# A decoder layer: the order of TensorE's transposes among the projections beside them

## The chip, the cores and the metric

The kernel runs on one core of a Trainium2 chip. The metric is the device time in microseconds, the median of three runs. A core has engines that work side by side, each through its own instructions in order: TensorE (PE, matmuls and transposes, results in PSUM), VectorE (DVE), ScalarE (ACT), GpSimd (POOL) and SyncE (SP, which issues DMAs). Semaphores make one wait for another.

## What is computed

A decoder layer on x of shape 4 x 512 x 512 with a context of the same shape, fp32. LN is a layer normalization over the last axis; there are 16 heads of 32.

```python
x = x + attn(LN(x))                 # causal self-attention, 16 heads
x = x + cross(LN(x), ctx, ctx)      # causal, no projections: keys and values are ctx
y = LN(x)
top2 = top_k(y @ W_gate.T, 2)
x = x + relu(y @ W_up.T) @ W_down.T + sum(softmax(top2)) * (y @ W_expert)

# attn: q, k, v = y @ w.T + b;  softmax(mask(q k.T / sqrt(32))) v;  then @ o_w.T + o_b
# cross: a masked score is -10000, not -inf; the rest as in attn, without weights
```

## The kernel before, in words

**Rounds.** The loop over b runs through the four batches; below, a round is one b. A round does self-attention, the output projection with the norms of the cross query, cross-attention, and the feed-forward. Activations that are contracted next must lie with the feature on the partitions, so normalized rows (tiles `made[0..3]`, 128 rows each) are turned by TensorE: `columns` (L243) issues four 128x128 transposes for each of two tiles into one pair of PSUM banks, and one ScalarE copy takes them to SBUF (`cqT`, the cross query, L257 with a scale; `fT`, the feed-forward input, L255).

**PSUM.** All PSUM tiles come from one pool of four buffers of two banks (`pair`, L65). A new tile takes a buffer that is free in the order of the program, and its first writer waits until the engine that read the old contents is done.

**The order of the work is written by hand** for TensorE, VectorE, ScalarE and GpSimd (L836): each runs what the program issues for it, in that order. SyncE's DMAs are issued by the same steps.

**Two passes of an attention.** `with_maxima` (L781) makes the first: for each of 4 groups of 4 heads, and in it for each of three units of query blocks, (0,1), (2) and (3), `Attention.maxima` (L267) computes scores (sm), ScalarE copies them (L292), GpSimd masks the diagonal (L298), and VectorE finds each row's largest value (`largest`, L310). `split` (L323) cuts the maxima of a group into bf16 parts, `rows` (L334) turns them: four transposes on TensorE (mt, L338) and a VectorE copy into `mrow` (L344). `attend` (L811) makes the second pass: scores again (sc, L370), minus the maxima by a matmul with `mrow` (L381), exponentials on ScalarE (L402), and the products with the values (pv, L429). It begins with units (0), (1), (2,3) of group 0. The last group's `rows` are called inside it.

**Filling.** Between the units of the first pass TensorE does other projections' matmuls: `steps`, through the generator `matmuls` (L775), which yields behind each matmul. How many come into a unit follows from the due time in L797: the total shared out by the units' costs and rounded. VectorE's work on a unit's scores (`jobs`) is issued one job behind each of the next unit's fill matmuls, and what is left behind the last. At a unit with block 3, from the second group on, `rows` of the group before is issued first, ahead of the fill, and its copy heads the jobs:

```python
            if i[-1] == NT - 1 and g > 0:
                jobs = a.rows(g - 1) + jobs
            due += total * cost[n] / sum(cost)
```

With the numbers of steps here, a unit with block 3 that calls `rows` gets 2 fill matmuls in the cross-attention of rounds 0 and 2 and in the self-attention of round 3, 2, 3 and 2 in the cross-attention of round 3, and 3 or 4 elsewhere. In the trace each fp32 matmul of the code is two instructions.

**What fills what.** In rounds 0 to 2 the query, key and value projections of the next batch (`query_key`, `value`) stand in the cross part, in round 3 the feed-forward of round 2: `gates` (share, which writes the logits' PSUM tile lg, L708, and gate), `ups`, `downs`; `experts` stand where they are put by L875 to L885. Round 3's self-attention is filled by one batch's experts alone.

**Around the change.** Behind the output projection come three steps, then all 16 transposes of the cross query, then the first pass:

```python
            run(steps[:3])
            norm_cross(e, made)
```

Behind the cross-attention, `filler` is value of the next batch (rounds 0 to 2) or experts (round 3): its first step, then `add_cross` (transposes tp_x, adding, norms), its other three steps, and `norm_ffn` (L681) with 16 transposes. The feed-forward's input tile in round 2 takes the buffer of `xnT`, which value reads.

Of the kernel before, what the change touches and what calls it, by code (L numbers as in the profile page):

```python
# [9 lines left out]
F32 = mybir.dt.float32  # L10
# [8 lines left out]
P = 128  # L19
# [7 lines left out]
def decoder_layer(  # L27
# [22 lines left out]
    B, S, D = x.shape  # L50
    NH = 16
    HD = D // NH
    NT = S // P
    NC = D // P
    HG = P // HD
    NE = wgate.shape[-1]
    SCALE = 1.0 / math.sqrt(HD)

    const = ctx.enter_context(tc.tile_pool(name="const", bufs=1))
    act = ctx.enter_context(tc.tile_pool(name="act", bufs=1))  # L60
# [4 lines left out]
    def pair(name):  # L65

        return ps.tile([P, 2, S], F32, tag="ps", name=name)


    def load_x(b):  # L70
        xb = act.tile([P, NT, D], F32, tag="x", name=f"x_{b}", bufs=2)
        src = x[b].rearrange("(t p) d -> p t d", p=P)
        for t in range(NT):
            queue = nc.scalar if b == 0 and t % 2 else nc.sync
            queue.dma_start(out=xb[:, t, :], in_=src[:, t, :])
        return xb
# [62 lines left out]
    for r in range(HG):  # L139
# [26 lines left out]
        fill=BIG,  # L166
# [6 lines left out]
    for n in range(2):  # L173
        t = const.tile([P, NT, P], BF16, name=f"parts{n}")
# [3 lines left out]
    def keep_warm(name, count):  # L178

        out = pair(name)  # L180
        for n in range(count):
            nc.tensor.matmul(
                out[:, 0, :P], lhsT=ident, rhs=ident, start=True, stop=True
            )
# [58 lines left out]
    def columns(srcs, dst, t, tp, scale=None, warm=0):  # L243

        for n, src in enumerate(srcs):
            if warm:
                keep_warm(f"warm_{t}_{n}", warm)
            for c in range(NC):
                nc.tensor.transpose(
                    tp[:, n, c * P : (c + 1) * P], src[:, c * P : (c + 1) * P], ident  # L250
                )
        to = dst[:, :, t * P : (t + 2) * P].rearrange("p c (n q) -> p c n q", q=P)
        come = tp.rearrange("p n (c q) -> p c n q", q=P)
        if scale is None:
            nc.scalar.copy(to, come)  # L255
        else:
            nc.scalar.mul(to, come, scale)  # L257
# [251 lines left out]
    def norm_in(b, given=None):  # L509

        e = Entry()
        e.b, e.x, e.xn_t = b, given, None
        src = x[b].rearrange("(t p) d -> p t d", p=P)

        def source(t):
            if given is not None:
                return given[:, t, :]
            xi = work.tile([P, D], F32, tag="xin", name=f"xin_{b}_{t}")
            nc.sync.dma_start(out=xi, in_=src[:, t, :])
            return xi  # L520

        made, norms = layernorms(source, f"a{b}")

        def turn(t):
            if e.xn_t is None:
                e.xn_t = act.tile([P, NC, S], F32, tag="xn_t", name=f"xnT_{b}")
            columns(
                [made[t], made[t + 1]],
                e.xn_t,
                t,  # L530
                pair(f"tp_a{b}_{t}"),
                warm=0 if b else 2,
            )

        return e, norms, [(lambda t=t: turn(t)) for t in (0, 2)]

    def add_bias(e):
        for t in range(NT):
            nc.gpsimd.tensor_tensor(e.x[:, t, :], e.x[:, t, :], bo_sb, ALU.add)
# [49 lines left out]
    def value(e):  # L589
        b, made = e.b, {}  # L590
        e.v = act.tile([P, NT, D], F32, tag="v", name=f"v_{b}")

        def one(t):
            if t % 2 == 0:
                made[0] = pair(f"pm_v{b}_{t}")
            yield from project(made[0][:, t % 2, :], e.xn_t, wv_sb, t)
            if t % 2 == 1:
                nc.vector.tensor_tensor(
                    e.v[:, t - 1 : t + 1, :],
                    made[0],  # L600
                    bv_sb.unsqueeze(1).to_broadcast([P, 2, D]),
                    ALU.add,
                )

        return [(lambda t=t: one(t)) for t in range(NT)]
# [47 lines left out]
        run(norms)  # L653
        return made

    def norm_cross(e, made):
        b = e.b
        e.cq_t = act.tile([P, NC, S], F32, tag="o_t", name=f"cqT_{b}")
        for t in (0, 2):
            columns(made[t : t + 2], e.cq_t, t, pair(f"tp_q{b}_{t}"), SCALE)  # L660

    def add_cross(e, a):
        b = e.b
# [14 lines left out]
        run(norms)  # L678
        return made

    def norm_ffn(e, made):  # L681
        b = e.b
        e.f_t = act.tile(
            [P, NC, S], F32, tag="f_t" if b != B - 2 else "xn_t", name=f"fT_{b}"
        )
        for t in (0, 2):
            columns(made[t : t + 2], e.f_t, t, pair(f"tp_f{b}_{t}"))

    def ffn(e):
        b, f_t, made = e.b, e.f_t, {}  # L690
# [79 lines left out]
    def run(steps):  # L770
        for step in steps:
            for _ in step() or ():
                pass

    def matmuls(steps):  # L775

        for step in steps:
            yield from step() or ()
            yield

    def with_maxima(steps, a, first=0, norms=()):  # L781


        norms = list(norms)
        run(steps[:first])
        fill = matmuls(steps[first:])
        total = sum(1 if step.__name__ in ("share", "gate") else NC for step in steps[first:])
        units = [(g, i) for g in range(NC) for i in ((0, 1), (2,), (3,))]
        cost = [sum(k + 1.5 for k in i) for _, i in units]
        done, due, jobs = 0, 0.0, []  # L790
        for n, (g, i) in enumerate(units):
            new = a.maxima(g, i)
            if norms and n % 2 == 0:
                new.append(norms.pop(0))
            if i[-1] == NT - 1 and g > 0:
                jobs = a.rows(g - 1) + jobs
            due += total * cost[n] / sum(cost)  # L797

            while done < round(due):
                next(fill, None)  # L800
                done += 1
                run(jobs[:1])
                jobs = jobs[1:]
            run(jobs)
            jobs = new
        for _ in fill:
            pass
        run(jobs)
        return NC - 1
# [26 lines left out]
    with tc.manual_schedule(engines=BY_HAND):  # L836
        e, norms, turns = norm_in(0, x0)
        keep_warm("warm", 12)
        run(norms)
        run(turns)  # L840
        nc.gpsimd.tensor_scalar(bqs_sb, bq_sb, SCALE, None, ALU.mult)
        add_bias(e)
        between_self = query_key(e) + value(e)
        skip, between_cross, ahead = 3, [], []
        for b in range(B):
            more = b + 1 < B
            sa = Attention(e.q_t, e.k_t, e.v, False, f"s{b}")
            norms, turns = [], []
            if more:
                after, norms, turns = norm_in(b + 1)  # L850
            late = with_maxima(between_self, sa, skip, norms)
            if b == B - 1:
                e.x = load_x(b)
            attend(sa, late)
            if b > 0:
                add_bias(e)
            made = out_projection(e, sa, context(e) + turns)
            steps = (query_key(after) if more else []) + between_cross
            run(steps[:3])
            norm_cross(e, made)  # L860
            ca = Attention(e.cq_t, e.ck_t, e.cv, True, f"c{b}")
            ca.e = e
            late = with_maxima(steps[3:], ca)
            if b + 2 < B:
                after.x = load_x(b + 1)
            attend(ca, late)
            if more:
                cvs[b + 1] = load_cv(b + 1)
            filler = value(after) if more else ahead
            run(filler[:1])  # L870
            made = add_cross(e, ca)
            run(filler[1:])
            norm_ffn(e, made)
            gates, ups, downs, experts = ffn(e)
            if b + 3 < B:  # L875
                between_self, between_cross = gates[:1] + ups + gates[1:] + downs, experts
            elif b + 2 < B:
                between_self, between_cross = gates[:1] + ups + gates[1:] + downs, []
                ahead = experts
            elif more:  # L880
                between_self, ahead = ahead, experts
                between_cross = gates[:1] + ups + gates[1:] + downs
            else:
                run(gates[:1] + ups + gates[1:])
                run(downs[:2] + experts[:2] + downs[2:] + experts[2:])  # L885
            skip = 0
            if more:
                e = after
# [48 lines left out]
```

## Time and profile before

| what | value |
|---|---|
| median of 3 runs | 830.17 us (830.14 to 830.2) |
| the profiled execution | 829.93 us |
| its span, first to last instruction | 828.2 us |
| TensorE busy | 813.8 us, 98% |
| VectorE busy | 547.0 us, 66% |
| ScalarE busy | 397.9 us, 48% |
| GpSimd busy | 297.8 us, 36% |
| granted TensorE clock | 0.999 |

How to read it: the page names engines PE, DVE, ACT and POOL. A row of a timeline is: start in us, length in us, engine, line, operation, output<-inputs, shape, number of instructions, and in brackets idle time of the engine ahead of it with what ended it. A row of waits is: total us, times, longest. Matmuls overlap, and a row's length reaches to the modelled end of its last one, so starts are the surer measure. L310 is line 310 of the kernel before.

### The profile page before, as it was taken

The page shows a single profiled execution, that of the slowest core. Times are in us where ns is not written, and L with a number is a line of the kernel's source. Part 1 is how long each engine was busy: PE and PEld are TensorE (multiplying, and loading weights), DVE is VectorE, ACT ScalarE, POOL GpSimd, SP SyncE. Part 2 cuts the span into 40 slices and gives each one's busy share as a digit, 9 for nine tenths or more (in the row PEclk, how much of TensorE's full clock was granted, in tenths as well). Part 3 has the DMA queues.
Part 4 walks back from the last instruction along what each step waited for, and adds up shares of the span by engine and source line. Part 5 has one row for each costly group of instructions (what it writes and reads, how often), then busy time and mean ns, then how long its engine had stood idle before and what let it go on. Part 6 is the DMA issues. An engine that isn't in the chain of part 4 may idle for free.

```text
span 828.2 us, 14453 instructions
## 1 busy us (share of the span) xinstructions
PE 813.8 (98%) x5800; PEld 369.4 (45%) x5800; DVE 547.0 (66%) x937; ACT 397.9 (48%) x502; POOL 297.8 (36%) x549
## 2 busy tenths in 40 slices
PE   9999999999999999999999999999998999999998
PEld 7344444345444454334534444434543444444443
DVE  2578736877678834687858863687779835887511
ACT  2456526761546515556054651676166714574110
POOL 4434512442334732234233471244233643333100
PEclk9999999999999999999999999999999999999999
DMA  9600000001010000030100000000102000000101
GB/s 340 232 27 15 1 1 1 2 2 51 5 35 13 2 1 1 0 103 2 51 14 13 2 2 0 1 2 2 53 16 72 18 1 0 1 2 2 51 0 51
DMA packets 13539, 24.54 MB, mean 30 GB/s; under 512 B 1952, under 2 KB 1952, under 8 KB 13472
## 3 DMA queue, kind: packets, MB, share of 16 engines
q1 hardware_dynamic: 13184, 23.09, 8.2%
q8 instruction: 45, 0.74, 0.4%
q10 hardware_dynamic: 288, 0.52, 0.2%
q14 instruction: 22, 0.18, 0.1%
HBM read 19.42 MB, written 4.19 MB: 29 GB/s over the span
## 4 chain that ended last, share of the span: by engine, by line
PE 92%; ACT 3%; DVE 3%; issue 2%; DMA 0%; POOL 0%; ACTq 0%
PE pm_qk L233 12%; PE pv_c L429 9%; PE pm_u L233 7%; PE pm_d L221 7%; PE pm_v L221 7%; PE pm_o L638 7%; PE pm_e L221 6%; PE pv_s L429 6%; PE sm_c L280 6%; PE sc_s L370 5%; PE sc_c L370 5%; PE sm_s L280 5%; PE sc_s L381 1%; DVE nm_s L310 1%; PE sc_c L381 1%
## 5 line engine op out<-in xcount | busy, mean ns | idle before, releaser
L310 DVE TENSOR_REDUCE nm_c<-s_c 128x2 f32<-128x256 f32 (+3 forms) x128 | 96.3, 810 | 36.6 <-POOL s_c L298 36.6
L310 DVE TENSOR_REDUCE nm_s<-s_s 128x2 f32<-128x256 f32 (+3 forms) x128 | 96.6, 810 | 28.1 <-POOL s_s L298 28.1
L292 ACT COPY s_s<-sm_s 128x768 f32<-128x768 f32 (+1 forms) x96 | 78.9, 874 | 67.2 <-PE sm_s L280 50.9
L292 ACT COPY s_c<-sm_c 128x768 f32<-128x768 f32 (+1 forms) x96 | 78.9, 875 | 48.8 <-PE sm_c L280 34.5
L402 ACT ACTIVATE pt_c<-sc_c 128x768 f32<-128x768 f32 (+1 forms) x96 | 78.6, 883 | 28.7 <-PE sc_c L381 24.8
L298 POOL TENSOR_SCALAR_AFFINE_SELECT s_c<-s_c 128x256 f32<-128x256 f32 (+1 forms) x96 | 46.7, 487 | 119.1 <-ACT s_c L292 118.1
L404 POOL TENSOR_SCALAR_AFFINE_SELECT pt_c<-pt_c 128x256 f32<-128x256 f32 (+1 forms) x96 | 56.7, 598 | 71.0 <-ACT pt_c L402 70.1
L298 POOL TENSOR_SCALAR_AFFINE_SELECT s_s<-s_s 128x256 f32<-128x256 f32 (+1 forms) x96 | 46.9, 491 | 96.7 <-ACT s_s L292 95.7
L458 DVE TENSOR_TENSOR sum_s<-sum_s,pt_s 128x512 f32<-128x512 f32 (+1 forms) x72 | 63.2, 915 | 7.4 <-PE pv_s L429 6.4
L221 PE MATMUL pm_d<-wdown_sb,hT 128*128 128x512 f32 x128 | 60.4, 607 | 0.0
L402 ACT ACTIVATE pt_s<-sc_s 128x768 f32<-128x768 f32 (+1 forms) x72 | 55.9, 838 | 8.9 <-PE sc_s L381 6.4
L221 PE MATMUL pm_e<-wexp_sb,fT 128*128 128x512 f32 x128 | 60.2, 605 | 0.0
L233 PE MATMUL pm_u<-fT,wup_sb 128*128 128x512 f32 x128 | 59.9, 608 | 0.0
L370 PE MATMUL sc_s<-qT,kT 32*128 32x128 f32 (+3 forms) x512 | 58.2, 467 | 0.9 <-ACT sum_s L402 0.9
L233 PE MATMUL pm_qk<-xnT,wk_sb 128*128 128x512 f32 x120 | 58.6, 610 | 0.0
L638 PE MATMUL pm_o<-wo_sb,oT_s 128*128 128x512 f32 x128 | 57.8, 596 | 0.0
L221 PE MATMUL pm_v<-wv_sb,xnT 128*128 128x512 f32 x128 | 57.6, 598 | 0.0
L233 PE MATMUL pm_qk<-xnT,wq_sb 128*128 128x512 f32 x120 | 57.4, 604 | 0.0
L404 POOL TENSOR_SCALAR_AFFINE_SELECT pt_s<-pt_s 128x256 f32<-128x256 f32 (+1 forms) x72 | 48.7, 681 | 21.0 <-ACT pt_s L402 19.8
L370 PE MATMUL sc_c<-cqT,ckT 32*128 32x128 f32 (+3 forms) x512 | 51.8, 467 | 0.9 <-ACT pt_c L402 0.9
L280 PE MATMUL sm_c<-ckT,cqT 32*128 32x512 f32 (+3 forms) x512 | 49.1, 467 | 1.2 <-ACT cqT L257 1.2
L280 PE MATMUL sm_s<-kT,qT 32*128 32x512 f32 (+3 forms) x512 | 48.1, 467 | 0.0
(148 smaller groups left out, 1186.2 us busy)
## 6 DMA issues: line engine op xcount, KB each, us to landing
cv<-in_ctx_dram SPq DMA_DIRECT2D x16, 256.0 KB, 4.1
out_dram<-x SPq DMA_DIRECT2D x16, 256.0 KB, 2.0
x<-in_x_dram SPq DMA_DIRECT2D x14, 256.0 KB, 4.7
xin<-in_x_dram SPq DMA_DIRECT2D x12, 256.0 KB, 2.7
wq_sb<-in_wq_dram SPq DMA_DIRECT2D x2, 512.0 KB, 6.0
wk_sb<-in_wk_dram SPq DMA_DIRECT2D x2, 512.0 KB, 7.7
wv_sb<-in_wv_dram SPq DMA_DIRECT2D x1, 1024.0 KB, 8.3
wo_sb<-in_wo_dram SPq DMA_DIRECT2D x1, 1024.0 KB, 9.9
```

The costliest lines, as they stand in the source:

```text
L221: nc.tensor.matmul(pm, lhsT=lhs_t[:, c, t * P : (t + 1) * P], rhs=w[:, c, :], start=(c == 0), stop=(c == NC - 1),)
L233: nc.tensor.matmul(pm, lhsT=w[:, c, f * P : (f + 1) * P], rhs=rhs_t[:, c, :], start=(c == 0), stop=(c == NC - 1),)
L280: nc.tensor.matmul(scs[r // 2][:, r % 2, at[i] : at[i] + (i + 1) * P], lhsT=self.q_t[h, g, i * P : (i + 1) * P], rhs=self.k_t[h, g, : (i + ...
L292: nc.scalar.copy(s[:, :, :N], scs[n][:, :, :N])
L298: nc.gpsimd.affine_select(out=diagonal, in_=diagonal, compare_op=ALU.is_ge, fill=NEG, base=0, pattern=[[0, 2 * len(blocks)], [-1, P]], cha ...
L310: nc.vector.tensor_reduce(self.nm[g][:, i, 2 * n : 2 * n + 2], made[n][:, :, at[i] : at[i] + (i + 1) * P], axis=AX.X, op=ALU.max, negate=True,
L370: nc.tensor.matmul(scs[r // 2][:, r % 2, at[j] : at[j] + S - j * P], lhsT=self.k_t[h, g, j * P : (j + 1) * P], rhs=self.q_t[h, g, j * P :] ...
L402: nc.scalar.activation(pt[:, :, :N], scs[n][:, :, :N], AF.Exp)
L404: nc.gpsimd.affine_select(out=diagonal, in_=diagonal, compare_op=ALU.is_ge, fill=0.0, base=0, pattern=[[0, 2 * len(blocks)], [1, P]], chan ...
L429: nc.tensor.matmul(pv[r * HD : (r + 1) * HD, u, j * P :], lhsT=ones if u else self.v[:, j, h * HD : (h + 1) * HD], rhs=pts[r // 2][:, r % ...
L458: nc.vector.tensor_tensor(to, to, pts[n][:, :, at[j] : at[j] + S - j * P], ALU.add)
L638: nc.tensor.matmul(pms[t // 2][:, t % 2, :], lhsT=a.out[:, c, t * P : (t + 1) * P], rhs=wo_sb[:, c, :], start=(c == 0), stop=(c == NC - 1),)
```

## The change

Three places are reordered; no operation is added or taken away.

- In `with_maxima`, `rows` of the group before is issued behind the unit's second fill matmul instead of ahead of the first; its VectorE copy then stands behind one job of the unit before.
- The cross query's transposes are issued in two halves of eight: the first behind two steps, the second behind the third.
- The feed-forward input's are issued in two halves too: the first behind 8 of the 12 matmuls of the filler's last three steps, the second behind 2 more, and the last 2 follow. In round 2 (`b == B - 2`) all 12 come first, as before.

```diff
-    def norm_cross(e, made):
-        b = e.b
-        e.cq_t = act.tile([P, NC, S], F32, tag="o_t", name=f"cqT_{b}")
-        for t in (0, 2):
-            columns(made[t : t + 2], e.cq_t, t, pair(f"tp_q{b}_{t}"), SCALE)
+    def norm_cross(e, made, t):
+        if t == 0:
+            e.cq_t = act.tile([P, NC, S], F32, tag="o_t", name=f"cqT_{e.b}")
+        columns(made[t : t + 2], e.cq_t, t, pair(f"tp_q{e.b}_{t}"), SCALE)
...
-    def norm_ffn(e, made):
+    def norm_ffn(e, made, t):
         b = e.b
-        e.f_t = act.tile(
-            [P, NC, S], F32, tag="f_t" if b != B - 2 else "xn_t", name=f"fT_{b}"
-        )
-        for t in (0, 2):
-            columns(made[t : t + 2], e.f_t, t, pair(f"tp_f{b}_{t}"))
+        if t == 0:
+            e.f_t = act.tile(
+                [P, NC, S], F32, tag="f_t" if b != B - 2 else "xn_t", name=f"fT_{b}"
+            )
+        columns(made[t : t + 2], e.f_t, t, pair(f"tp_f{b}_{t}"))
...
-            if i[-1] == NT - 1 and g > 0:
-                jobs = a.rows(g - 1) + jobs
             due += total * cost[n] / sum(cost)
 
-            while done < round(due):
+            for k in range(round(due) - done):
                 next(fill, None)
                 done += 1
+                if k == 1 and i[-1] == NT - 1 and g > 0:
+                    jobs = a.rows(g - 1) + jobs
                 run(jobs[:1])
                 jobs = jobs[1:]
             run(jobs)
...
-            run(steps[:3])
-            norm_cross(e, made)
+            run(steps[:2])
+            norm_cross(e, made, 0)
+            run(steps[2:3])
+            norm_cross(e, made, 2)
...
-            run(filler[1:])
-            norm_ffn(e, made)
+
+            fill = matmuls(filler[1:])
+            for t, k in ((0, 8), (2, 2)) if b != B - 2 else ((0, 12), (2, 0)):
+                for _ in range(k):
+                    next(fill)
+                norm_ffn(e, made, t)
+            for _ in fill:
+                pass
```

## The prediction

> **What bounds the kernel now.** I read the page first, then TensorE's waits, then the timelines around the waits that it names, each one engine at a time. The page:
>
> ```profile
> span 828.2 us, 14453 instructions
> PE 813.8 (98%) x5800; PEld 369.4 (45%) x5800; DVE 547.0 (66%) x937; ACT 397.9 (48%) x502; POOL 297.8 (36%) x549
> PE 92%; ACT 3%; DVE 3%; issue 2%; DMA 0%; POOL 0%; ACTq 0%
> ```
>
> TensorE is busy 98% of the span and carries 92% of the chain that ended last. The granted clock is full in all 40 slices. So the time is TensorE's own work plus its waits, and an edit pays where a wait of TensorE ends sooner. The waits by line:
>
> ```profile
> PE mt_s L338 <- ACT s_s L292: 2.2, 2, 1.1
> PE mt_s L338 <- DVE parts L332: 1.9, 2, 1.7
> PE lg L708 <- ACT fT L255: 1.7, 3, 1.1
> PE sm_c L280 <- ACT cqT L257: 1.2, 4, 0.3
> ```
>
> These four rows are just the places that the change touches: mt is the transpose of maxima, lg reads the feed-forward input fT, sm_c reads the cross query cqT. They sum to 7.0 us, but "idle" counts only from the modelled end of the last matmul. I therefore compare starts: what a block of TensorE takes until the next block starts, with and without the wait.
>
> ```profile
> 125.49 1.91 PE L249 MATMUL tp_q<-ident,xn_q 128*128 128x128 f32 x16
> 127.69 0.94 PE L280 MATMUL sm_c<-ckT,cqT 32*128 32x128 f32 x16 [0.29 <-ACT cqT L257]
> ...
> 229.75 1.14 PE L280 MATMUL sm_s<-kT,qT 32*128 32x512 f32 x8
> 231.99 0.38 PE L338 MATMUL mt_s<-identb,parts 128*128 128x128 bf16 x4 [1.10 <-ACT s_s L292]
> ...
> 602.93 1.91 PE L249 MATMUL tp_f<-ident,xn_f 128*128 128x128 f32 x16
> 604.77 0.94 PE L280 MATMUL sm_s<-kT,qT 32*128 32x128 f32 x16
> 605.64 1.13 PE L221 MATMUL pm_e<-wexp_sb,fT 128*128 128x512 f32 x2
> ...
> 608.61 1.14 PE L280 MATMUL sm_s<-kT,qT 32*128 32x512 f32 x8
> 609.68 1.98 PE L221 MATMUL pm_e<-wexp_sb,fT 128*128 128x512 f32 x4
> 611.59 0.94 PE L280 MATMUL sm_s<-kT,qT 32*128 32x128 f32 x16
> ...
> 615.43 1.14 PE L280 MATMUL sm_s<-kT,qT 32*128 32x512 f32 x8
> 616.50 0.40 PE L338 MATMUL mt_s<-identb,parts 128*128 128x128 bf16 x4
> 616.74 1.94 PE L221 MATMUL pm_e<-wexp_sb,fT 128*128 128x512 f32 x4
> 618.60 0.94 PE L280 MATMUL sm_s<-kT,qT 32*128 32x128 f32 x16
> ```
>
> Unhindered, 16 transposes take 1.84 us to the next scores (602.93 to 604.77), 8 scores of the widest block 1.07 to whatever follows, projection (608.61) or mt (615.43), and the 16 scores of blocks 0 and 1 take 0.87 (604.77). At 125.49 the transposes take 2.20, at 229.75 the scores take 2.24. A projection matmul of the code is two instructions here, 0.43 us each.
>
> **Cross query in halves (four rounds).** Nothing is added: the same 16 transposes and two copies, with query(1) (8 instructions, 3.43 us) between the halves. Transposes behind a projection and a projection behind transposes start at the plain pitch (0.43 and 0.11), so the split is free on TensorE. The first half's copy then lies beside query(1), and only blocks 0 and 1 of the first scores, which read that half, follow at once. Gain 2.20 - 1.84 = 0.36 in rounds 0 to 2. Cover: the norms. In round 0 the third projection starts about 122.06; the second normalized tile was ready at 119.24 and the last at 122.51, while the second half starts at about 126.4. What is late next: the second copy, from about 127.2 to 128.3, before the scores of block 2 at 130.1. In round 3 the projections are share, up0 | up1, and four buffers of PSUM are all in use: the first half is covered by 0.4 us only (second tile at 685.44, transposes at 685.86), and ScalarE's Relu of up1 (1.03, at 689.59 before) comes ahead of the second copy (0.97), whose buffer the next up needs: 690.37 + 1.03 + 0.97 = 692.4 against 692.49 before. I take 0.10 there (ends 0 and 0.36). Sum 1.18.
>
> **Feed-forward input in halves.** Rounds 0 and 1: 16 instructions of value, half, 4, half, 4 (1.72 us). The wait at lg was 212.82 - 211.60 = 1.22 against 0.87, so 0.35 each. The second copy (0.97) now ends before the scores do. Cover for the halves: tiles ready at 205.00 and 208.28, halves at 206.3 and 208.9. VectorE's second add of v waits for matmuls that end 1.75 later, so 209.96 becomes about 211.7, its 1.22 still ends ahead of the maxima at 214.21. Round 2 keeps the old order: 0. Round 3, where lg follows directly: 781.01 - 777.96 = 3.05 against 1.84, so 1.21; the last four expert instructions (1.72) cover the copy. Its tiles (773.2, 776.5) precede the halves (774.5, 777.1). Sum 0.70 + 1.21 = 1.91. No DMA changes its place in SP's queue, no instruction its place on POOL: the moved steps issue transposes and ScalarE copies alone.
>
> **Transposes of maxima.** 24 of the 32 groups (the eight last ones, inside the attention, stay). Each issues four transposes on TensorE and one VectorE copy.
> - Removed waits: rounds 1 and 2 of self-attention, 2.24 - 1.07 = 1.17 twice (229.75, 433.00), 2.34. There mt wants the PSUM buffer of the scores just written, free when ScalarE's first copy ends at 231.9; two matmuls later is 229.75 + 1.07 + 1.82 = 232.64, so nothing is left.
> - Price of the place: a projection behind scores starts slower than one behind transposes. 4 of them take 1.91 (609.68 to 611.59), behind mt 1.86 (616.74 to 618.60). After the change the first projection stands behind scores, and where more projections follow the second run still stands behind mt. With four instructions in the unit: mt 0.24 + 1.91 instead of 0.24 + 1.86, 0.05 more; with six or more 0.10 more, since both slow starts are paid. Rounding of the due times gives 11 units with four and 13 with more. The three of round 3's self-attention are reckoned below: 8 x 0.05 + 13 x 0.10 = 1.70 lost.
> - Not shown: mt directly behind a fp32 projection, and scores behind mt. Nearest rows: 0.43 for transposes tp_q behind a projection (the plain pitch, nothing lost), 0.15 for pv behind mt. I take nothing extra, being nearest to tp_q; the ends are -0.05 (mt's own slower first pitch goes) and +0.10 (the slow start of a projection behind scores), so -1.2 to +2.4 for 24.
> - VectorE's order: a largest of the unit before now precedes the copy, the other follows. Queued behind the waiting copy are that second largest, the next unit's and split, for which the next mt waits two units later.
>
> ```profile
> 226.06 1.93 DVE L310 TENSOR_REDUCE nm_s<-s_s 128x2 f32<-128x256 f32 x4
> 232.41 0.42 DVE L344 COPY mrow_s<-mt_s 128x512 bf16<-128x512 bf16 x1 [4.42 <-PE mt_s L338]
> 232.75 1.80 DVE L310 TENSOR_REDUCE nm_s<-s_s 128x2 f32<-128x768 f32 x2
> ```
>
> VectorE idles 4.42 us ahead of this copy with the maxima ready; half of the 1.80 moves into that gap, and the copy waits 0.7 us longer (232.83 + 0.25 against 232.41). No wait for TensorE follows: its next scores there start at about 233.9, and the copy has freed its buffer at 233.5.
> - Round 3's self-attention has 16 projection matmuls to fill its units, where the others have 34 or 36, and VectorE sets its pace. The waits 625.24 - 622.44 - 1.07 = 1.73 and 632.59 - 631.19 - 1.07 = 0.33 go, since TensorE passes two matmuls first. But the first two score units of the attention then want buffers that VectorE frees: the expert sums (L761, 636.20 before) and the copy, now behind them at about 636.5. So the wait of nearly 2 us returns at the second score unit (L370), and only ScalarE's earlier exponentials give something: the third unit waited until 638.06 and would come at about 637.6. I take a gain of 0.4 (ends -0.3, the copy's lateness, and +1.9, the waits less 0.14).
>
> The Trainium skill, "TensorEngine Tiling (Array Packing)", Key Properties, says that a change of tiling mode drains TensorE. The scores use quarter-height tiles, mt and projections the whole array, and the number of changes stays; by that rule the place is free and the 1.70 falls away. The trace shows equal 1.07 behind the scores, which agrees, but also the slower start, which the sum keeps.
>
> **Sum.** 1.18 + 1.91 + 2.34 + 0.40 - 1.70 = 4.13. The profiled execution took 829.93 (span 828.2 and 1.7 around it), so 825.80; it lies 0.24 below the median 830.17, from which I subtract: 826.0.
>
> **The rivals.**
> - Place free: a slow start behind scores is not added, because the second weight load finds its time beside mt. For it: behind tp_q no slow start is seen. Against: 1.91 and 1.86 both hold a slow first start, and behind mt there still is one. 826.0 - 1.7 = 824.3. The rule of the Trainium skill's "TensorEngine Tiling (Array Packing)" above would give this time.
> - Absorbed by ScalarE. In all eight attentions the third score unit waits 0.2 us for exponentials; if that chain sets the start of each, every gain ahead of one is taken back, and only the last feed-forward's 1.21 is left: 829.0. For it: these waits, and ScalarE runs without a gap from 160.80 to 165.55. Against: ScalarE idled 2.31 us for the scores in front of the exponentials in round 0's self-attention, so TensorE sets them.
> - Slower: the copy frees mt's PSUM buffer too late. Where no projection follows mt (11 units), the next scores come 0.15 us behind the last transpose, but the copy ends 0.68 behind it (41.42 to 42.10). If those scores are given that buffer, each waits about 0.58: 11 x 0.58 = 6.4, 826.0 + 6.4 = 832.4. It decides from 4.13 / 11 = 0.38 each. For it: only four buffers. Against: scores take two, a projection one, mt the fourth; if buffers go round in turn the next scores get those of the last scores, which ScalarE has emptied by then.
>
> **How the numbers follow.** A measurement of this kernel tells about 0.2% (1.7 us) from no change, so 828.5 to 831.8 is "same". Forecast 0.60, place free 0.10, absorbed 0.16, buffer 0.14. The forecast's own range is 824.3 (round 3's waits all gained) to 828.4 (all 24 changeovers at +0.10). The 8-in-10 range reaches from 823.5 (place free, part of round 3) to 829.0 (absorbed) and leaves out the buffer's 0.14 and some tails. Faster 0.69, same 0.17, slower 0.14.
>
> **What would show it.** Right: the four wait rows at L338, L708 and L280 gone or down to 0.1, tp_q's second half of 8 transposes about 0.96 before sm_c; pm, mt, pm behind the widest scores with no idle; each of the 24 units 0.05 to 0.10 longer where it had no wait; in round 3 a new wait at L370 for VectorE of 1.5 to 2 us near 634. Wrong: idle of TensorE before L280 behind mt released by the copy L344 (the buffer), larger waits at L370 for ScalarE (absorbed), a pitch behind mt above 0.6 (changeover).

## The result

The changed kernel takes 825.07 us (median of 6 runs, 825.01 to 825.29) against 830.07 for the kernel before (6 runs, 829.89 to 830.2): ratio 0.9941, 95% interval 0.9928 to 0.9953, 5.0 us faster. The prediction was 826.0. The profiled execution took 825.04, its span is 823.3 instead of 828.2.

The page of the changed kernel, span, engines and the chain that ended last:

```profile
span 823.3 us, 14456 instructions
PE 813.3 (99%) x5800; PEld 368.8 (45%) x5800; DVE 544.6 (66%) x937; ACT 398.0 (48%) x502; POOL 298.3 (36%) x549
PE 94%; DVE 3%; ACT 1%; issue 1%; DMA 0%; POOL 0%; ACTq 0%
```

TensorE's busy time fell by 0.5 us only; what went is its idle time. Its waits:

```profile
PE warm L182 <- POOL ident masks.py:199: 1.5, 1, 1.5
PE sc_c L370 <- ACT pt_c L402: 1.3, 6, 0.2
PE sc_s L370 <- DVE x L760: 1.3, 1, 1.3
PE tp_a L249 <- DVE xn_a L208: 0.8, 2, 0.5
PE sc_s L370 <- ACT sum_s L402: 0.6, 3, 0.2
PE pm_e L221 <- DVE x L760: 0.4, 1, 0.4
```

All four rows that the prediction shows of before are gone (mt twice, lg, sm_c). Two are new, both for VectorE's expert sums (L760 here, L761 before): 1.3 us ahead of an attention's second score unit, and 0.4 us ahead of an expert matmul. The scores' waits for exponentials at L370 hardly changed, 1.3 + 0.6 us where they were 0.9 + 0.9. The tp_a row lies in the first 10 us, ahead of every place that moved; there the two traces are level again within 0.1 us. Timelines of TensorE in the changed kernel, round 0's cross query and round 1's transposes of maxima:

```profile
122.27 1.04 PE L249 MATMUL tp_q<-ident,xn_q 128*128 128x128 f32 x8
123.14 3.60 PE L233 MATMUL pm_qk<-xnT,wq_sb 128*128 128x512 f32 x8
126.58 1.04 PE L249 MATMUL tp_q<-ident,xn_q 128*128 128x128 f32 x8
127.54 0.94 PE L280 MATMUL sm_c<-ckT,cqT 32*128 32x128 f32 x16
...
229.37 1.14 PE L280 MATMUL sm_s<-kT,qT 32*128 32x512 f32 x8
230.44 1.98 PE L233 MATMUL pm_u<-fT,wup_sb 128*128 128x512 f32 x4
232.26 0.39 PE L338 MATMUL mt_s<-identb,parts 128*128 128x128 bf16 x4
232.49 1.08 PE L233 MATMUL pm_u<-fT,wup_sb 128*128 128x512 f32 x2
233.49 0.94 PE L280 MATMUL sm_s<-kT,qT 32*128 32x128 f32 x16
```

The second half takes 0.96 us to the scores (126.58 to 127.54), with no idle time in brackets. ScalarE's copies of the halves start at 123.62 and 127.65, so the scores of blocks 0 and 1, which read the first half alone, begin ahead of the second copy. The unit with mt takes 233.49 - 229.37 = 4.12 instead of 5.19 (229.75 to 234.94).

The logits' matmuls lg of round 3, which read the feed-forward input, before and below in the changed kernel:

```profile
777.96 1.91 PE L249 MATMUL tp_f<-ident,xn_f 128*128 128x128 f32 x16
781.01 1.07 PE L708 MATMUL lg<-fT,wgate_sb 128*32 128x512 f32 x8 [1.14 <-ACT fT L255]
```

```profile
773.45 1.04 PE L249 MATMUL tp_f<-ident,xn_f 128*128 128x128 f32 x8
774.32 1.88 PE L221 MATMUL pm_e<-wexp_sb,fT 128*128 128x512 f32 x4
776.13 1.07 PE L707 MATMUL lg<-fT,wgate_sb 128*32 128x512 f32 x8
```

Following the same matmul through both traces gives where the time went. The third column is how much earlier (minus) or later it starts in the changed kernel; the differences from row to row are the gains and prices.

| matmul | before, us | changed kernel | moved by that stage |
|---|---|---|---|
| last mt of round 0, self | 75.65 | +0.22 | 0.27 lost (it began 0.05 ahead) |
| first cross scores, round 0 | 127.69 | -0.15 | 0.36 won at the cross query |
| tp_x, round 0 | 197.72 | -0.05 | 0.10 lost at three mt |
| lg, round 0's feed-forward | 212.82 | -0.38 | 0.35 won at the feed-forward input |
| scores behind the first mt of round 1 | 234.94 | -1.45 | 1.07 won: the wait, less 0.10 |
| last mt of round 1, self | 265.57 | -1.26 | 0.2 lost at two mt |
| first cross scores, round 1 | 317.61 | -1.62 | 0.36 won |
| tp_x, round 1 | 400.97 | -1.34 | 0.28 lost at three mt |
| lg, round 1's feed-forward | 416.07 | -1.68 | 0.34 won |
| last mt of round 2, self | 468.82 | -2.56 | 1.06 won, 0.2 lost |
| first cross scores, round 2 | 520.86 | -2.92 | 0.36 won |
| tp_x, round 2 | 590.88 | -2.81 | 0.11 lost at three mt |
| last mt of round 3, self | 643.54 | -3.67 | 0.86 won |
| up2 in round 3's cross part | 692.49 | -3.71 | 0.04 won at the cross query |
| lg, round 3's feed-forward | 781.01 | -4.88 | 1.21 won at the feed-forward input, the rest even |

### The profile page after: what moved, and what is told of

It reads as the page before. It is cut to its first block, busy times and chain, and to the rows that moved or that the text cites. A ratio compares the mean times of both kernels' runs of the same rounds, so it can differ in the third digit from the quotient of the medians.

```text
span 823.3 us, 14456 instructions
## 1 busy us (share of the span) xinstructions
PE 813.3 (99%) x5800; PEld 368.8 (45%) x5800; DVE 544.6 (66%) x937; ACT 398.0 (48%) x502; POOL 298.3 (36%) x549
## 4 chain that ended last, share of the span: by engine, by line
PE 94%; DVE 3%; ACT 1%; issue 1%; DMA 0%; POOL 0%; ACTq 0%
PE pm_qk L233 13%; PE pv_c L429 9%; PE pm_d L221 7%; PE pm_u L233 7%; PE pm_v L221 7%; PE pm_o L638 7%; PE pm_e L221 6%; PE pv_s L429 6%; PE sm_c L280 6%; PE sc_s L370 6%; PE sc_c L370 5%; PE sm_s L280 5%; DVE nm_s L310 1%; PE sc_s L381 1%; PE sc_c L381 1%; PE tp_x L666 1%
## 5 line engine op out<-in xcount | busy, mean ns | idle before, releaser
L370 PE MATMUL sc_s<-qT,kT 32*128 32x128 f32 (+3 forms) x512 | 57.4, 466 | 1.9 <-DVE x L760 1.3
L370 PE MATMUL sc_c<-cqT,ckT 32*128 32x128 f32 (+3 forms) x512 | 51.5, 467 | 1.3 <-ACT pt_c L402 1.3
L280 PE MATMUL sm_c<-ckT,cqT 32*128 32x512 f32 (+3 forms) x512 | 49.4, 468 | 0.0
L280 PE MATMUL sm_s<-kT,qT 32*128 32x512 f32 (+3 forms) x512 | 48.1, 467 | 0.0
```

The source lines that it names most:

```text
L280: nc.tensor.matmul(scs[r // 2][:, r % 2, at[i] : at[i] + (i + 1) * P], lhsT=self.q_t[h, g, i * P : (i + 1) * P], rhs=self.k_t[h, g, : (i + ...
L370: nc.tensor.matmul(scs[r // 2][:, r % 2, at[j] : at[j] + S - j * P], lhsT=self.k_t[h, g, j * P : (j + 1) * P], rhs=self.q_t[h, g, j * P :] ...
```

## The experiments

All times are medians, the ratios are to the kernel before, run beside each set, with their 95% intervals. That kernel came at 829.85 to 830.07 from set to set, so a difference of 0.2 us between kernels of two sets tells little. Theory: TensorE sets the time, each wait that is taken out of its order is won in full, and each place among the scores has a small price. Rivals: ScalarE or VectorE sets the pace ahead of each attention; VectorE's order, not TensorE's, made the gain; the halving, not what follows it, made the feed-forward's gain; the copy keeps a PSUM buffer too long.

**Each part alone.** The edits are those of the change's diff, one part at a time.

> The transposes of maxima alone are moved; the cross query and the feed-forward input stay whole. If the parts are independent, the sites add up: 2.34 us of waits gone in rounds 1 and 2, about 0.9 gained in round 3's self-attention, about 1.4 paid at the 21 other units: 1.8 us under the kernel before, 828.3. If ScalarE or VectorE sets the pace ahead of each attention and the change gains only through the feed-forward, no gain: 830.

> Only the cross query is turned in halves. Independent parts: 0.36 us in three rounds and 0.04 in the fourth, 1.1 us under the kernel before, 829.0, and the wait of sm_c for cqT gone from three rounds. If the exponentials take the gain back in each attention: 830.

> Only the feed-forward input is turned in halves. Independent parts: 0.35 + 0.35 + 1.21 = 1.9 us under the kernel before, 828.2. If only what lies behind the last attention counts: 1.2 us, 828.9.

| part alone | us | ratio | against 830.04 |
|---|---|---|---|
| transposes of maxima | 828.25 | 0.9978 (0.9969 to 0.9987) | -1.79 |
| cross query in halves | 828.85 | 0.9986 (0.9977 to 0.9995) | -1.19 |
| feed-forward input in halves | 828.14 | 0.9978 (0.9969 to 0.9987) | -1.90 |

They add up to 4.88, the whole change won 4.97 over this median. Nothing that one part wins is taken back by another. The gain of the cross query lies wholly ahead of attentions, and all of it is kept: the rival by which ScalarE absorbs such gains falls.

**Moving the maxima only where they waited.** Five units of 24 move, in the self-attention of rounds 1, 2 and 3:

```diff
-            if i[-1] == NT - 1 and g > 0:
+            if i[-1] == NT - 1 and g > 0 and n not in late:
                 jobs = a.rows(g - 1) + jobs
...
+                if k == 1 and n in late:
+                    jobs = a.rows(g - 1) + jobs
...
+            late = with_maxima(between_self, sa, skip, norms, ((), (5,), (5,), (5, 8, 11))[b])
```

> As the changed kernel, but the transposes of maxima move only at five units: the one with a wait in rounds 1 and 2 of self-attention, and the three of round 3's; the other 19 stay ahead of the fill. If the place behind two matmuls costs 0.09 us where projections follow and 0.035 where none do, 11 and 8 such units give back 1.0 + 0.3: 823.8. If the place is free: 825.1.

824.03 us (0.9928, 0.9915 to 0.994), 1.04 below the changed kernel; the profiled spans, 822.1 and 823.3, differ by 1.2. The first unit with mt in round 0, in this kernel (at the head of the unit) and below in the changed one (behind two matmuls):

```profile
40.07 1.14 PE L280 MATMUL sm_s<-kT,qT 32*128 32x512 f32 x8
41.14 0.40 PE L338 MATMUL mt_s<-identb,parts 128*128 128x128 bf16 x4
41.38 1.08 PE L233 MATMUL pm_qk<-xnT,wq_sb 128*128 128x512 f32 x2
42.29 1.88 PE L233 MATMUL pm_qk<-xnT,wk_sb 128*128 128x512 f32 x4
44.10 0.94 PE L280 MATMUL sm_s<-kT,qT 32*128 32x128 f32 x16
```

```profile
40.11 1.14 PE L280 MATMUL sm_s<-kT,qT 32*128 32x512 f32 x8
41.18 1.12 PE L233 MATMUL pm_qk<-xnT,wq_sb 128*128 128x512 f32 x2
42.14 1.02 PE L233 MATMUL pm_qk<-xnT,wk_sb 128*128 128x512 f32 x2
43.00 0.39 PE L338 MATMUL mt_s<-identb,parts 128*128 128x128 bf16 x4
43.22 1.08 PE L233 MATMUL pm_qk<-xnT,wk_sb 128*128 128x512 f32 x2
44.23 0.94 PE L280 MATMUL sm_s<-kT,qT 32*128 32x128 f32 x16
```

The same eight scores, four transposes and six projection instructions take 4.03 us in the first and 4.12 in the second, which has two slow starts instead of one: the first projection behind the scores is 0.53 ahead of the next, the first behind mt 0.48 in both kernels, against 0.43 otherwise. So the place has a price where nothing waited: 0.09 a unit, and 0.035 where mt stands last and only one slow start is paid (0.53 instead of 0.48, less the 0.01 by which mt itself is quicker behind a projection). The rival "place free" falls.

**Feed-forward: halves, or the matmuls behind?** Two edits of one tuple in the changed kernel: the first leaves no matmul (the tail) behind the second half, the second puts both halves together ahead of the tail.

```diff
-            for t, k in ((0, 8), (2, 2)) if b != B - 2 else ((0, 12), (2, 0)):
+            for t, k in ((0, 8), (2, 4)) if b != B - 2 else ((0, 12), (2, 0)):
...
-            for t, k in ((0, 8), (2, 2)) if b != B - 2 else ((0, 12), (2, 0)):
+            for t, k in ((0, 10), (2, 0)) if b != B - 2 else ((0, 12), (2, 0)):
```

> As the changed kernel, but the second half of the feed-forward input comes behind all twelve matmuls, so that none is left behind it. If the matmuls behind the second half are what hides its copy, round 3's lg waits about 1 us again and rounds 0 and 1 about 0.1 each (there the scores still stand between): 826.2. If the halving itself is what pays (one copy of 0.97 instead of two in a row): 825.1 to 825.4.

> As the changed kernel, but all 16 transposes of the feed-forward input come together behind ten of the twelve matmuls, and two follow. If the matmuls behind them are what pays, their 1.72 us hide both copies, no wait at lg: 825.1. If the halving pays, lg waits 0.3 us in rounds 0 and 1 and 0.3 to 1.2 in round 3: 826 to 827.

Without the tail 827.05 (0.9964, 0.9951 to 0.9978), with both halves together ahead of the tail 825.22 (0.9943, 0.993 to 0.9955). With the halving alone the feed-forward's 1.9 us are lost again; with the tail alone they are kept, but for 0.15 that is too small to tell from none. The run without a tail, TensorE at lg in round 3, and ScalarE's copies there:

```profile
775.99 1.04 PE L249 MATMUL tp_f<-ident,xn_f 128*128 128x128 f32 x8
778.13 1.07 PE L707 MATMUL lg<-fT,wgate_sb 128*32 128x512 f32 x8 [1.10 <-ACT fT L255]
```

```profile
772.75 1.01 ACT L255 COPY fT<-tp_f 128x1024 f32<-128x1024 f32 x1 [15.16 <-PE tp_f L249]
777.06 1.01 ACT L255 COPY fT<-tp_f 128x1024 f32<-128x1024 f32 x1 [3.30 <-PE tp_f L249]
```

The second copy starts when the last transpose has ended and takes its 1.01, though the first was made 4 us earlier. In the kernel before, where both follow in a row, they take 1.93 from 779.04: eight transposes (0.87) take nearly as long as a copy, so the second queued for no more than 0.1. The expectation of 0.1 us for rounds 0 and 1 was wrong: by the starts lg waits 0.31 in each again, of 0.35 before the change.

The cross query has no such pair of runs. There the second half stands directly ahead of the scores, and the first of them read only the first half, so the halving may well be needed; all 16 transposes ahead of query(1) were not tried.

**One matmul instead of two.** In the changed kernel `k == 1` becomes `k == 0`; the copy then heads VectorE's jobs, as before the change.

> As the changed kernel, but the transposes of maxima come behind one matmul, and VectorE's copy heads its jobs again, as before the change. If the buffer of the scores is what they waited for, 0.2 us of the wait is left in rounds 1 and 2 each, and the 11 units with two matmuls pay 0.05 more: 825.9. If VectorE's order (one largest ahead of the copy) made the gain, about 1.8 us are lost: 826.9.

826.13 us (0.9955, 0.9942 to 0.9967), 1.06 above the changed kernel. Round 1, TensorE:

```profile
229.51 1.14 PE L280 MATMUL sm_s<-kT,qT 32*128 32x512 f32 x8
230.58 1.13 PE L233 MATMUL pm_u<-fT,wup_sb 128*128 128x512 f32 x2
231.75 0.38 PE L338 MATMUL mt_s<-identb,parts 128*128 128x128 bf16 x4
```

mt comes 1.17 us behind the first projection, which with its slow start would take 0.96: the 0.2 that is left of the wait. It starts 2.24 us behind the scores' start, just as in the kernel before (229.75 to 231.99): the buffer is free at that moment wherever mt stands in the order. By the starts these two waits give 0.4 of the 1.06, and each unit with two fill matmuls pays about 0.06 more.

**The copy first, on VectorE.** The changed kernel, but the jobs of these units are held until the copy is issued:

```diff
-                run(jobs[:1])
-                jobs = jobs[1:]
+                if k > 0 or i[-1] < NT - 1 or g == 0:
+                    run(jobs[:1])
+                    jobs = jobs[1:]
```

> As the changed kernel, transposes of maxima behind two matmuls, but the copy heads VectorE's jobs in these units, so that VectorE idles until the transposes. If TensorE's waits made the gain, rounds 0 to 2 are unchanged, and round 3's self-attention, which VectorE paces, loses what it won, up to 0.9 us: 825.5 to 826. If VectorE's order made the gain of all rounds: 826.9 and waits of TensorE for VectorE in rounds 0 to 2.

825.28 us (0.9944, 0.9932 to 0.9957), 0.2 above the changed kernel, though VectorE now idles longer ahead of its copies. VectorE's waits, in the changed kernel and below in this one:

```profile
DVE mrow_s L344 <- PE mt_s L338: 14.5, 7, 3.7
...
DVE mrow_c L344 <- PE mt_c L338: 13.6, 9, 3.7
```

```profile
DVE mrow_s L344 <- PE mt_s L338: 18.7, 7, 5.1
DVE mrow_c L344 <- PE mt_c L338: 17.8, 10, 5.5
```

VectorE idles 8.4 us more ahead of these copies, and the kernel takes 0.2 us more, which is hardly clear of the spread. In the traces TensorE's starts in rounds 0 to 2 stay within 0.04 us of the changed kernel's, but for 0.08 at the very start, and round 3's self-attention loses 0.1, not the 0.4 to 0.9 expected. VectorE's order is not what made the gain.

**The copy last.** The changed kernel with `jobs = jobs + a.rows(g - 1)`.

> As the changed kernel, but VectorE's copy of the turned maxima comes behind all jobs of the unit before, so that it frees mt's buffer about 0.9 us later. If the four buffers go round in turn and the next scores take those of the last scores, nothing changes outside round 3: 825.1 to 825.5. If the next scores need mt's buffer, TensorE waits ahead of L280 for L344 at most of the 24 units: 830 or more.

825.66 us (0.9949, 0.9936 to 0.9961), 0.6 above the changed kernel and 0.2 above the top of what was expected. No row of the waits stands ahead of L280. TensorE's rows for the copy are at L370 alone, the second score unit of an attention:

```profile
PE sc_s L370 <- DVE x L760: 0.8, 1, 0.8
...
PE sc_c L370 <- DVE mrow_c L344: 0.3, 1, 0.3
PE sc_s L370 <- DVE mrow_s L344: 0.3, 1, 0.3
PE sc_c L370 <- DVE x L760: 0.2, 1, 0.2
```

So a score unit does take mt's buffer, but not the next one. Four of the six second units in rounds 0 to 2 start 0.3 to 0.5 us later, that of round 3's cross-attention up to 0.9, and the third units are level again. Only round 3's self-attention, where VectorE is behind, keeps a delay of 0.64 to the end; 0.24 of it comes at two score units of L280, the second ones behind mt, which start 0.06 us behind the end of the copy, too short a wait for a row. The buffer rival has its place there, and at the change's own timing no row for the copy appears.

**Round 3's self-attention.** Two kernels from the one that moves five units. In the first its last unit lets the expert sums and the copy go ahead of both maxima:

```diff
-                run(jobs[:1])
-                jobs = jobs[1:]
+                if k > 0 or n != 11 or n not in late:
+                    run(jobs[:1])
+                    jobs = jobs[1:]
```

> As the kernel that moves the transposes only at the five units with waits, and in round 3's last unit the expert sums and the copy go ahead of both maxima in VectorE's order. If the 1.26 us wait of the second score unit (L370) is for the expert sums alone, it shrinks by about 0.9, of which ScalarE's exponentials give 0.5 to 0.9 through: 823.1 to 823.5. If VectorE's backlog sets the end of this stage whatever its order: 824.0.

The second moves nothing in round 3, `((), (5,), (5,), ())[b]`:

> As the kernel that moves the transposes of maxima only where they waited, but without the three units of round 3's self-attention. If round 3 gains 0.86 us by them, as the starts of the changed kernel read: 0.9 above 824.0, 824.9. If only the 0.40 of the prediction: 824.4. If the new waits for the expert sums take all of it back: 824.0.

823.62 us (0.9924, 0.991 to 0.9937) and 824.83 us (0.9938, 0.9924 to 0.9951). Round 3's three moved units are worth 0.80, not 0.40. With the sums first the wait shrinks:

```profile
PE pm_e L221 <- DVE x L760: 0.4, 1, 0.4
PE sc_s L370 <- DVE x L760: 0.4, 1, 0.4
```

The row of 1.3 becomes 0.4, and 0.4 of those 0.9 reach the end: 823.62 against 824.03. By the starts the second score unit gains 0.86 on the kernel that moves five units, and from the second group on 0.36 is left, a little under the 0.5 to 0.9 expected.

**Round 3's cross query.** On top of the kernel with the sums first, the second half comes ahead of up1's last matmul, so that its copy stands ahead of the Relu on ScalarE:

```diff
-            run(steps[2:3])
+            third = matmuls(steps[2:3])
+            for _ in range(NC if more else NC - 1):
+                next(third)
             norm_cross(e, made, 2)
+            run([lambda: third])
```

> As the run before it, and in round 3 the second half of the cross query comes one matmul earlier, ahead of up1's last, so that its copy stands ahead of the Relu on ScalarE. If the Relu is what kept round 3 from gaining more than 0.04 us, about 0.3 more: 0.2 to 0.3 under the run before it. If it is the number of PSUM buffers, no change.

823.56 us (0.9924, 0.9911 to 0.9936), no change beside 823.62. ScalarE there:

```profile
685.49 1.02 ACT L257 ACTIVATE cqT<-tp_q 128x1024 f32<-128x1024 f32 x1 [2.43 <-PE tp_q L249]
686.41 1.02 ACT L700 ACTIVATE hT<-pm_u 128x1024 f32<-128x1024 f32 x1
687.38 1.50 ACT L292 COPY s_c<-sm_c 128x768 f32<-128x768 f32 x2
```

The two have changed places, and the scores' copy follows behind both as before. The order of the two is not the cause. In both kernels the first scores start in two parts, and the later part starts 0.05 to 0.06 us behind the end of whichever of the two comes first: 686.47 behind 686.42, the end of the Relu, with the sums first, and 686.57 behind 686.51, the end of the copy, here. That is how a wait for a freed buffer would look, with all four in use; a fifth was not tried, so it stays open.

The fastest kernels are this one and the one with the sums first, 823.6 us, 1.5 below the changed kernel.

## Why the prediction was right, step by step

- **Cross query in halves, 1.18 predicted.** Alone it won 1.19; in the trace 0.36 in rounds 0 to 2 and 0.04 instead of 0.10 in round 3, where the scores start in two parts, as if waiting for a buffer; the prediction had only the next up waiting there.
- **Feed-forward input, 1.91 predicted.** Alone 1.90; 0.35, 0.34 and 1.21 at lg. The step credited it to the copies hidden by the last matmuls, which the two runs bear out.
- **Removed waits of maxima, 2.34 predicted.** Both waits are gone, and the run with one matmul leaves just the 0.2 that the buffer's time gives.
- **Price of the place, 1.70 predicted, about 1.4 measured.** This term was a little too large: 0.09 and 0.035 a unit instead of 0.10 and 0.05, since the 0.01 that mt saves was left out of the sum. The unseen changeovers, mt behind a projection (0.43) and scores behind mt (0.15), came as the nearest rows had them.
- **Round 3's self-attention, 0.40 predicted, 0.80 to 0.86 measured.** This is the term that was mis-sized most. The mechanism was as told: the wait came back at L370, for the expert sums and not for the maxima, at 633.0 with 1.26 us. Its size was less than the 1.5 to 2 given, because VectorE was ahead of what the prediction assumed. VectorE's expert sums before, then in the changed kernel, and TensorE's wait there:

```profile
618.71 1.41 DVE L761 SCALAR_TENSOR_TENSOR x<-pm_e,rw,x 128x512 f32<-128x512 f32 x2 [1.23 <-PE pm_e L221]
...
634.79 1.41 DVE L761 SCALAR_TENSOR_TENSOR x<-pm_e,rw,x 128x512 f32<-128x512 f32 x2
```

```profile
615.71 1.41 DVE L760 SCALAR_TENSOR_TENSOR x<-pm_e,rw,x 128x512 f32<-128x512 f32 x2 [0.52 <-PE pm_e L221]
...
631.56 1.40 DVE L760 SCALAR_TENSOR_TENSOR x<-pm_e,rw,x 128x512 f32<-128x512 f32 x2
```

```profile
633.02 0.92 PE L370 MATMUL sc_s<-qT,kT 32*128 32x384 f32 x6 [1.26 <-DVE x L760]
```

Ahead of the first sums VectorE's idle time fell from 1.23 to 0.52 us, a largest now standing ahead of them. The changed kernel comes to this stage 2.81 us early. On the clock of before its last sums thus end at 632.96 + 2.81 = 635.77, where the prediction kept the 636.20 of before, and the part of the third score unit that waited until 638.06 starts at 634.26 + 2.81 = 637.07 without a wait, where the prediction had 637.6. That VectorE's shorter idle time is the whole cause was not tried by itself.

- **Place free and absorbed by ScalarE** are refuted by the five-unit run and by the cross query alone. **The buffer** was the rival with a true mechanism, at a place and a time where it costs nothing. Its price was also added up a little too high: by its own row the copy ends 0.68 - 0.15 = 0.53 us behind the scores' start, not 0.58, which makes 5.8 us and not 6.4.

The sum was 0.9 us too small: about 0.45 from round 3, 0.3 from the place, and 0.1 from the median of before, which came 0.1 lower this time. The rest is too small to tell apart.

## What to carry to other kernels

Where one engine is busy 98% of the time, take the starts of its blocks and compare a block that waits with the same block that doesn't. Outside round 3's attentions that gave the gain of each removed wait within 0.05 us, while the idle column had about 0.07 less each time (1.14 against 1.21 at round 3's lg). Put other work between a transpose and the reader of its copy, as long as the copy takes; in the feed-forward, splitting the transposes by itself won nothing. And move only what waits: the same reordering at 19 places without a wait cost 1.0 us here.

## What was not expected of the hardware

- An instruction of a fp32 projection of 512 columns needs 0.53 us to the next one where it stands behind scores (41.18 in the changed kernel), 0.48 behind four bf16 transposes (43.22), and 0.43 in a row or behind eight fp32 transposes (123.14). So the four bf16 transposes between projections cost their own time and 0.05, and the eight fp32 ones their own time alone.
- Four bf16 transposes behind a projection are as cheap as behind scores: 0.22 us to the next projection (43.00 to 43.22 in the changed kernel) against 0.24 (41.14 to 41.38 in the one that moves five units).
- Eight 128x128 fp32 transposes (0.87) and the 1.01 us copy of their result run at nearly the same pace, which is why two copies in a row hardly queue (1.93 for both at 779.04 before).
